# Graph attention on one core: two key blocks of scores in a row, then the sums of two blocks

## Chip, cores, metric

The kernel runs on one core of a Trainium2 chip. The metric is the device time of one execution in microseconds (us); lower is better. One core has TensorE (matrix products, into PSUM), VectorE, ScalarE, GpSimd (POOL in the profile) and the queues that issue DMAs, SyncE's (SP) among them.

## Reference

Four graph layers over 4096 nodes with 128 features, each followed by a residual and a layer norm. The change concerns the second layer, a masked attention with four heads of 32 features:

```
q, k, v = x @ Wq + bq, x @ Wk + bk, x @ Wv + bv      # (4096, 4 heads, 32)
attn  = q . k / sqrt(32)                             # per head, 4096 x 4096
e     = exp(attn) where adj != 0, else 0             # (softmax, its maximum taken off)
out   = (e @ v) / (row sum of e)
x_r   = x @ Ws + bs
beta  = sigmoid([out, x_r, out - x_r] @ Wb)
x     = layernorm(x + beta * x_r + (1 - beta) * out)
```

`adj` is a 4096 x 4096 matrix of zeros and ones in float32, symmetric, with about 1.6% ones. The other three layers use the same matrix in other ways and are not touched.

## The kernel before

`attention_unshifted` computes the second layer without taking the maximum off (a test on the sizes of q and k guards this). The queries are cut into 8 outer blocks of 512 (`NS`, index `I`), the keys into 32 blocks of 128 (`NT`, index `jb`). A list `seq` holds all 256 pairs (I, jb) in order.

For each pair there are two steps:

- `scores(I, jb)`: for two heads at a time, TensorE computes the transposed scores of 128 keys by 512 queries into a PSUM tile `ps` (pool `ps_s`, three buffers; a tile holds two heads; L1994). ScalarE takes the exp of the tile into the SBUF tile `e` (pool `ep`, three buffers; L2001). When all four heads are there, VectorE multiplies `e` with the mask, which it makes from a bfloat16 block `at` of the adjacency matrix (L2003).
- `sums(I, jb)`: TensorE multiplies the masked `e` with the values, which carry a column of ones for the row sums, and accumulates over the 32 key blocks in two PSUM tiles `pv` (pool `ps_v`; L2020). Two heads share a tile, one in its lower and one in its upper 64 partitions. A product of plain float32 appears in the profile as two instructions, so one key block has eight of them.

The order on every engine's queue is the order in which the program is written (`manual_schedule`); within it the framework picks the buffers and sets the waits. The main loop runs over n with `LEAD = 2`: it issues the scores of pair n + 2 and then the sums of pair n. TensorE's queue thus alternates: four score matmuls, eight sum matmuls. Other work is placed in the loop by hand:

- `load` (SyncE's queue, L1959) brings the mask block for four key blocks, one ahead, into one of two buffers.
- `row` (ScalarE's queue, L1970) loads half of an adjacency row block; `degree` (ScalarE, L1976) sums it, for the third layer; `look` (VectorE, L1985) tests some of these rows. They come at every fourth key block.
- `stack` (POOL's queue, L2181) brings keys and queries into the layout of the score matmuls. In the first outer block a one-element copy `pace` (POOL, L2127) on a masked `e` delays it.
- `ending(I)` finishes an outer block after its last sums. ScalarE copies the two `pv` tiles to SBUF (L2033); TensorE transposes them in two portions into tiles `pto` of the pool `ps_s` (L2043), one portion into each tile; VectorE divides (L2044 to L2050), forms the gate and the layer norm, with a few tiny functions on ScalarE. It is a generator: the loop takes one portion of it, `next(rest)`, after the sums of each following key block.

Of the kernel before, what the change touches and what calls it, by code (L numbers as in the profile page):

```python
# [1643 lines left out]
class Fast(Net):  # L1644
# [296 lines left out]
    def attention_unshifted(self, VA, KS, QS, at0, stack, R, wb):  # L1941

        nc, tc, N, NT, NS, D, X = self.nc, self.tc, self.N, self.NT, self.NS, self.D, self.X
        NH, C = 4, D // 4
        W = C + 1
        with ExitStack() as ctx:
            rot = ctx.enter_context(tc.tile_pool(name="rotf", bufs=1))
            natp = ctx.enter_context(tc.tile_pool(name="natf", bufs=2))
            atp = ctx.enter_context(tc.tile_pool(name="atf", bufs=1))
            ep = ctx.enter_context(tc.tile_pool(name="ef", bufs=3))  # L1950
            ps_s = ctx.enter_context(tc.tile_pool(name="ps_s", bufs=3, space=PSUM))
            ps_v = ctx.enter_context(tc.tile_pool(name="ps_v", bufs=1, space=PSUM))
            st = {("at", 0, 0): at0, "look": []}
# [3 lines left out]
            def load(I, J):  # L1957
                at = st["at", I, J] = ats[J % 2]
                nc.sync.dma_start(out=at, in_=self.block(I, J))  # L1959
# [3 lines left out]
            def row(n):  # L1963

                if n < len(halves):
                    i, k = halves[n]
                    h, c = N // 2, slice(k * N // 2, (k + 1) * N // 2)
                    st["row"] = n
                    st["nat"] = natp.tile([P, h], F32, tag="nat", name="nat")
                    nc.scalar.dma_start(out=st["nat"], in_=self.adj[i * P : (i + 1) * P, c])  # L1970

            def degree():
                n = st["row"]
                i, k = halves[n]
                nat = st["nat"]
                nc.scalar.activation(nat, nat, AF.Identity, accum_out=self.deg2[:, k, i : i + 1])  # L1976
                row(n + 1)
                if i % 4 > 1:
                    st["look"] = [nat[:, b * N // 4 : (b + 1) * N // 4] for b in range(2)]

            def look():

                if st["look"]:
                    a = st["look"].pop(0)
                    nc.vector.scalar_tensor_tensor(  # L1985
                        a, a, 0.0, a, op0=ALU.not_equal, op1=ALU.not_equal, accum_out=self.mark()
                    )

            def scores(I, jb):
                e = ep.tile([P, NH, S], F32, tag="e", name="e")  # L1990
                for h2 in range(0, NH, 2):
                    p = ps_s.tile([P, 2, S], F32, tag="s", name="ps")
                    for h in range(2):
                        nc.tensor.matmul(  # L1994
                            p[:, h, :],
                            lhsT=KS[:, h2 + h, jb * P : (jb + 1) * P],
                            rhs=QS[I % 2][:, h2 + h, :],
                            start=True,
                            stop=True,
                        )  # L2000
                    nc.scalar.activation(e[:, h2 : h2 + 2, :], p, AF.Exp)  # L2001
                at = st["at", I, jb // 4]
                nc.vector.scalar_tensor_tensor(  # L2003
                    e,
                    at[:, jb % 4, :].unsqueeze(1).to_broadcast([P, NH, S]),
                    0.0,
                    e,
                    op0=ALU.not_equal,
                    op1=ALU.mult,
                )  # L2010
                st["e", I, jb] = e

            def sums(I, jb):
                e = st.pop(("e", I, jb))
                if jb == 0:
                    st["po"] = [ps_v.tile([P, S], F32, tag=f"pv{a}", name=f"pv{a}") for a in range(2)]
                for h in range(NH):
                    g = 64 * (h % 2)
                    o = (jb * NH + h) * W
                    nc.tensor.matmul(  # L2020
                        st["po"][h // 2][g : g + 64, :],
                        lhsT=VA[:, o : o + 64],
                        rhs=e[:, h, :],
                        start=(jb == 0),
                        stop=(jb == NT - 1),
                        skip_group_check=True,
                    )
# [77 lines left out]
            seq = [(I, jb) for I in range(NS) for jb in range(NT)]  # L2105
            LEAD = 2
            rest = iter(())
            d = self.deg
            with tc.manual_schedule():
                load(0, 1)  # L2110
                row(0)
                for n in range(-LEAD, len(seq)):
                    if n + LEAD < len(seq):
                        I, jb = seq[n + LEAD]
                        if jb % 4 == 0:
                            m = n + LEAD + 4
                            if m < len(seq) and (m // 4) > 1:
                                load(m // NT, m % NT // 4)

                        if jb % 4 == 3 and (I or jb > 8) or I == NS - 1 and jb in (13, 17):  # L2120
                            look()
                            degree()
                        if I == 0 and jb % 4 == 0 and jb // 4 + 2 < NS:
                            c = jb // 4 + 2
                            if jb:

                                nc.gpsimd.tensor_copy(pace, st["e", I, jb - 1][0:1, 0, 0:1])  # L2127
                            stack(1, KS[:, :, c * S : (c + 1) * S], c)
                        if jb == 3 and 0 < I < NS - 1:
                            stack(0, QS[(I + 1) % 2], I + 1)  # L2130
                        scores(I, jb)
                        if n == -LEAD:
                            nc.scalar.preload_act_table_set("natural_log_exp_and_others")
                        if jb % 4 < 2:
                            look()
                    if n >= 0:
                        I, jb = seq[n]
                        sums(I, jb)
                        next(rest, None)
                        if jb == NT - 1:  # L2140
                            for _ in rest:
                                pass
                            rest = ending(I)
                            next(rest)
                for _ in range(2):
                    look()
                for _ in rest:
                    pass
# [430 lines left out]
```

## Time and profile before

| | |
|---|---|
| median of 3 runs | 2046.96 us (2040.15 to 2052.23) |
| profiled execution, its own time | 2050.21 us |
| its span in the trace | 2048.4 us |
| TensorE busy, of the span | 1900.9 us, 93% |
| VectorE busy | 1736.6 us, 85% |
| ScalarE busy | 1328.8 us, 65% |
| mean granted TensorE clock | 0.954 |

The stage of the change reaches from about 790 to 1590 us of the span. In the profile PE is TensorE's matmuls, PEld its weight loads, DVE is VectorE, ACT is ScalarE, SP is SyncE; a trailing q marks a queue's own instruction, such as the issue of a DMA. L1994 is line 1994 of the kernel. A group's row gives the tiles written and read, the shapes, the number of instructions, their busy time, the mean length of one, and how long the engine was idle just before them and on whose account. The ends of matmuls are modelled, so starts are the firmer numbers for TensorE.

### The profile page before, as it was taken

The numbers are of one execution on the slowest core, as the hardware profiler recorded it, in microseconds if no ns is written. First come the engines' busy times: TensorE is split into PE (matmuls) and PEld (weight loads), VectorE is DVE, ScalarE is ACT, GpSimd is POOL, SyncE is SP. The second block draws the span as 40 slices with busy tenths as digits, with TensorE's granted clock in tenths as the row PEclk, the third lists the DMA queues.
The fourth block names the chain that finished last, engine by engine and source line by source line (L and its number), as shares of the span: only waits on it lengthen the run. The fifth ranks groups of instructions, "written<-read, shape, count | busy, mean of one in ns | idle before, by whom it ended". The sixth has DMA issues, their size and how long they took to land.

```text
span 2048.4 us, 23818 instructions
## 1 busy us (share of the span) xinstructions
PE 1900.9 (93%) x8648; PEld 978.9 (48%) x8680; DVE 1736.6 (85%) x2685; ACT 1328.8 (65%) x1681; POOL 171.4 (8%) x269
## 2 busy tenths in 40 slices
PE   4789999999997788999999999999999799999997
PEld 4257766666666454333333333333333344444443
DVE  6579999998988946789999999999999777778986
ACT  5589999999997723777787777778787322210000
POOL 2211112111100221300000000000000000000000
PEclk8569999999999998999999999999999999999999
DMA  3488989899825977853535453545343799934441
GB/s 101 49 139 147 155 167 157 155 163 168 144 93 191 363 277 223 199 152 132 144 124 146 136 150 134 144 133 155 124 139 118 290 396 373 340 116 156 155 148 43
DMA packets 138064, 350.22 MB, mean 171 GB/s; under 512 B 13196, under 2 KB 56364, under 8 KB 125648
## 3 DMA queue, kind: packets, MB, share of 16 engines
q1 hardware_dynamic: 82944, 230.27, 32.3%
q0 software_dynamic: 45632, 50.69, 20.1%
q10 hardware_dynamic: 9360, 67.64, 9.9%
q8 instruction: 70, 1.15, 0.2%
q14 instruction: 58, 0.48, 0.1%
HBM read 371.54 MB, written 44.12 MB: 203 GB/s over the span
## 4 chain that ended last, share of the span: by engine, by line
PE 49%; DVE 24%; ACT 16%; DMA 6%; issue 4%; SPq 0%; POOL 0%; another core or an unknown queue 0%; ACTq 0%; DVEq 0%; POOLq 0%
PE pv L2020 11%; PE pa L1573 9%; DVE e L2003 9%; PE pa L2372 7%; PE ps L1994 6%; ACT e L2001 4%; PE pz L1775 3%; DMA up<-adjb 3%; DVE nat L1985 2%; ACT w L1792 2%; PE pi L1859 2%; PE pj L1874 2%; ACT s L1815 2%; ACT y L1811 2%; ACT y L1807 1%
## 5 line engine op out<-in xcount | busy, mean ns | idle before, releaser
L2003 DVE SCALAR_TENSOR_TENSOR e<-at,e 128x2048 f32<-128x2048 bf16 x256 | 582.6, 2286 | 77.3 <-ACT e L2001 76.7
L2001 ACT ACTIVATE e<-ps 128x1024 f32<-128x1024 f32 x512 | 492.9, 1024 | 150.6 <-PE ps L1994 121.6
L2020 PE MATMUL pv<-e,VA 128*64 128x512 f32 x2048 | 497.6, 607 | 6.7 <-DVE e L2003 5.7
L1994 PE MATMUL ps<-QS,KS 128*128 128x512 f32 x1024 | 314.8, 425 | 9.1 <-ACT e L2001 8.5
L1994 PEld LDWEIGHTS ps<-QS,KS 128*128 128x128 f32 x1024 | 170.9, 189 | 236.5 <-ACT e L2001 177.4
L2020 PEld LDWEIGHTS pv<-e,VA 128*64 128x64 f32 x2048 | 125.1, 136 | 250.2 <-issue 214.4
L1573 PE MATMUL pa<-w,Y 128*128 128x512 f32 x448 | 195.3, 594 | 0.0
L1775 PE MATMUL pz<-HT 128*128 128x512 f32 x288 | 171.8, 681 | 15.0 <-DVE w L1847 10.2
L1570 DVE SCALAR_TENSOR_TENSOR w<-rho,col,ring 128x512 f32<-128x512 f32 x224 | 162.7, 746 | 22.3 <-PE pa L1573 9.7
L2372 PE MATMUL pa<-ring,Y 128*128 128x512 bf16 x750 | 172.7, 384 | 8.7 <-ACT Y L2353 6.7
L1859 PE MATMUL pi<-HA,w 128*128 128x129 f32 x1152 | 156.6, 286 | 6.5 <-ACT s L1815 5.3
L1859 PEld LDWEIGHTS pi<-HA,w 128*128 128x128 f32 x1152 | 143.3, 199 | 18.2 <-issue 10.2
L1573 PEld LDWEIGHTS pa<-w,Y 128*128 128x128 f32 x448 | 83.8, 190 | 105.9 <-issue 80.3
L1976 ACT ACTIVATE nat<-nat 128x2048 f32<-128x2048 f32 x64 | 122.6, 1915 | 2.8 <-DMA nat<-in_adj_dram 2.8
L1874 PE MATMUL pj<-HA,w 128*128 128x129 f32 x896 | 120.7, 293 | 3.4 <-DVE X L1888 2.4
L2372 PEld LDWEIGHTS <-Y 128*128 128x128 bf16 x768 | 75.4, 99 | 100.9 <-ACT Y L2353 9.7
L1784 DVE TENSOR_SCALAR t<-pz 128x512 f32<-128x512 f32 x144 | 93.6, 682 | 30.2 <-PE pz L1778 30.2
L1874 PEld LDWEIGHTS pj<-HA,w 128*128 128x128 f32 x896 | 112.8, 205 | 11.2 <-issue 6.8
L1823 DVE SCALAR_TENSOR_TENSOR t<-t,s 128x2048 f32<-128x2048 f32 x36 | 82.3, 2286 | 13.4 <-ACT s L1815 13.4
L1792 ACT ACTIVATE w<-di,dr 128x512 f32<-128x512 f32 x144 | 90.6, 707 | 1.5 <-DMA di<-rows 1.5
L2336 DVE SCALAR_TENSOR_TENSOR nat<-nat 128x2048 f32<-128x2048 f32 x32 | 73.1, 2287 | 20.5 <-DMA nat<-in_adj_dram 20.5
L1847 DVE TENSOR_TENSOR w<-w,ptz 128x512 f32<-128x512 f32 x112 | 73.4, 681 | 18.7 <-PE ptz L1842 17.3
(410 smaller groups left out, 2343.1 us busy)
## 6 DMA issues: line engine op xcount, KB each, us to landing
nat<-in_adj_dram ACTq DMA_DIRECT2D x64, 1024.0 KB, 5.1
ring<-adjb SPq DMA_DIRECT2D x128, 512.0 KB, 4.7
ad<-in_adj_dram SPq DMA_DIRECT2D x36, 1024.0 KB, 9.4
adjb<-in_adj_dram POOLq DMA_DIRECT2D x64, 512.0 KB, 11.4
nat<-in_adj_dram SPq DMA_DIRECT2D x32, 1024.0 KB, 7.5
at<-adjb SPq DMA_DIRECT2D x63, 512.0 KB, 3.5
low<-adjb SPq DMA_DIRECT2D x36, 512.0 KB, 5.1
up<-adjb SPq DMA_DIRECT2D x28, 512.0 KB, 6.6
```

Source lines behind the costliest of these rows:

```text
L1570: nc.vector.scalar_tensor_tensor(w, rho[:, I * S : (I + 1) * S], col[:, 0, j : j + 1], at[:, jb, :], op0=ALU.max, op1=ALU.mult)
L1573: nc.tensor.matmul(pa, lhsT=F[:, j, :], rhs=w, start=False, stop=(j == NT - 1), skip_group_check=True)
L1775: nc.tensor.matmul(pz, lhsT=HT[:, j * P : (j + 1) * P], rhs=HT[:, I * S : (I + 1) * S], start=True, stop=False)
L1792: nc.scalar.activation(w[:, jb, :], st[p]["d"][k], AF.Sigmoid, bias=dr[:, 4 * J + jb : 4 * J + jb + 1])
L1859: nc.tensor.matmul(row[I, "po"][ib // 2][:, ib % 2, :], lhsT=st[p]["w0"][:, jb, ib * P : (ib + 1) * P], rhs=HA[:, 4 * J + jb, :], start=False,
L1874: nc.tensor.matmul(pj[:, a, :], lhsT=st[p]["w1"][:, ib, jb * P : (jb + 1) * P], rhs=HA[:, 4 * I + ib, :], start=(ib == 0), stop=(ib == 3),)
L1976: nc.scalar.activation(nat, nat, AF.Identity, accum_out=self.deg2[:, k, i : i + 1])
L1994: nc.tensor.matmul(p[:, h, :], lhsT=KS[:, h2 + h, jb * P : (jb + 1) * P], rhs=QS[I % 2][:, h2 + h, :], start=True, stop=True,)
L2001: nc.scalar.activation(e[:, h2 : h2 + 2, :], p, AF.Exp)
L2003: nc.vector.scalar_tensor_tensor(e, at[:, jb % 4, :].unsqueeze(1).to_broadcast([P, NH, S]), 0.0, e, op0=ALU.not_equal, op1=ALU.mult,)
L2020: nc.tensor.matmul(st["po"][h // 2][g : g + 64, :], lhsT=VA[:, o : o + 64], rhs=e[:, h, :], start=(jb == 0), stop=(jb == NT - 1), skip_gro ...
L2372: nc.tensor.matmul(st["pa"], lhsT=parts[k][:, j, :], rhs=at[:, jb, :], start=(I > 0 and j == k == 0), stop=(j == NT - 1 and k == 2), skip_ ...
```

## The change

The loop over n takes steps of two. One pass issues the scores of pairs n + 2 and n + 3, each with the loads, row sums and looks that stood ahead of and behind it, and then the sums of pairs n and n + 1. The pool of the masked exps gets a fourth buffer. `next(rest)` is still taken twice for two key blocks: once between the two score blocks (after that with even jb), and once after the two blocks of sums.

```
-            ep = ctx.enter_context(tc.tile_pool(name="ef", bufs=3))
+            ep = ctx.enter_context(tc.tile_pool(name="ef", bufs=4))
...
-                for n in range(-LEAD, len(seq)):
-                    if n + LEAD < len(seq):
-                        I, jb = seq[n + LEAD]
+                for n in range(-LEAD, len(seq), 2):
+                    for I, jb in seq[n + LEAD : n + LEAD + 2]:
                         if jb % 4 == 0:
-                            m = n + LEAD + 4
+                            m = I * NT + jb + 4
                             if m < len(seq) and (m // 4) > 1:
                                 load(m // NT, m % NT // 4)
...
                         scores(I, jb)
-                        if n == -LEAD:
+                        if I == jb == 0:
                             nc.scalar.preload_act_table_set("natural_log_exp_and_others")
                         if jb % 4 < 2:
                             look()
-                    if n >= 0:
-                        I, jb = seq[n]
+                        if n >= 0 and jb % 2 == 0:
+                            next(rest, None)
+                    if n < 0:
+                        continue
+                    for I, jb in seq[n : n + 2]:
                         sums(I, jb)
-                        next(rest, None)
-                        if jb == NT - 1:
-                            for _ in rest:
-                                pass
-                            rest = ending(I)
-                            next(rest)
+                    next(rest, None)
+                    if jb == NT - 1:
+                        for _ in rest:
+                            pass
+                        rest = ending(I)
+                        next(rest)
```

## Prediction

> **What bounds the kernel now.** The change lies in the second layer, so I first took the busy time by stretches to see which engine that stage runs on, then the costliest groups, then TensorE's timeline in a steady stretch. The table of stretches gives the stage as 790 to 1590 us of the span; one row stands for its middle (columns: stretch, length, then busy time and instructions by engine, TensorE's clock, DMA share, GB/s):
>
> ```profile
> core 0: us, PE busy (x) PEld busy (x) DVE busy (x) ACT busy (x) POOL busy (x), PEclk, DMA share, GB/s
> 1100.00:1200.00 100.00, 99.24 (x401) 38.19 (x400) 92.54 (x110) 79.23 (x91) 2.15 (x4) 1.00 0.46 138
> ```
>
> TensorE is never idle, at full clock; VectorE has 7% left, ScalarE 21%, the DMA engines half. But a busy TensorE need not be at its best pace. The groups (engine, operation, tiles, count, busy us, mean ns of one, idle before):
>
> ```profile
> L2003 DVE SCALAR_TENSOR_TENSOR e<-at,e 128x2048 f32<-128x2048 bf16 x256 | 582.6, 2286 | 77.3 <-ACT e L2001 76.7
> L2001 ACT ACTIVATE e<-ps 128x1024 f32<-128x1024 f32 x512 | 492.9, 1024 | 150.6 <-PE ps L1994 121.6
> L2020 PE MATMUL pv<-e,VA 128*64 128x512 f32 x2048 | 497.6, 607 | 6.7 <-DVE e L2003 5.7
> L1994 PE MATMUL ps<-QS,KS 128*128 128x512 f32 x1024 | 314.8, 425 | 9.1 <-ACT e L2001 8.5
> ```
>
> A key block is thus four score matmuls, two exps, one masking and eight sum matmuls. TensorE's timeline (start, length) shows the beat, and narrow windows of it the starts inside one beat:
>
> ```profile
> 1284.38 1.94 PE L2020 MATMUL pv<-e,VA 128*64 128x512 f32 x8
> 1286.25 1.20 PE L1994 MATMUL ps<-QS,KS 128*128 128x512 f32 x4
> 1287.38 1.94 PE L2020 MATMUL pv<-e,VA 128*64 128x512 f32 x8
> ...
> 1284.86 0.60 PE L2020 MATMUL pv<-e,VA 128*64 128x512 f32 x2
> 1285.72 0.60 PE L2020 MATMUL pv<-e,VA 128*64 128x512 f32 x2
> 1286.25 0.50 PE L1994 MATMUL ps<-QS,KS 128*128 128x512 f32 x1
> 1286.59 0.63 PE L1994 MATMUL ps<-QS,KS 128*128 128x512 f32 x2
> 1286.82 0.63 PE L1994 MATMUL ps<-QS,KS 128*128 128x512 f32 x2
> 1287.06 0.40 PE L1994 MATMUL ps<-QS,KS 128*128 128x512 f32 x1
> ```
>
> One block is 3.00 us, sums start to sums start. Within it a score follows a score after 0.235 us and a pair of sums a pair after 0.43. Around each turn it is slower: first to second score 0.34, last score to sums 0.32, first to second pair of sums 0.48, last pair to scores 0.53. Against the plain steps (0.235, 0.235, 0.43, 0.43) that is 0.105 + 0.085 + 0.05 + 0.10 = **0.34 us for each round of two turns**.
>
> An outer row block (32 key blocks) takes 98.35 us (sums at 1177.05 and 1275.40 us stand at the same place), so 2.35 over 32 x 3.00: 0.97 at jb 3 and 5, where the transposes of `ending` run, and the rest small stalls at jb 13, 21, 25 and 29, where VectorE or ScalarE is late (3.22, 3.28, 3.19 and 3.74 us for a block).
>
> **What the Trainium skill says.** TensorEngine Tiling (Array Packing), Key Properties: changing the tiling mode drains TensorE. Scores use 128 columns, sums 64, so each turn is such a change; the 0.34 us agrees with it. PSUM — Partial Sum Buffer, The four PSUM rules: one matmul output fills at most one of 8 banks. A score tile of 2 x 512 f32 is two banks; three of them and the two sums are all eight, so no fourth score buffer exists. ScalarE: Activation LUTs, What ACT_TABLE_LOAD costs: an ACTIVATE with immediates takes 186 + 0.833 N ns, and neighbours overlap by about 93. For N = 1024 that is 1039; the trace has 1024, and 0.92 from start to start.
>
> **The change part by part.** Time 0 is the first score matmul of a two-block group.
>
> *Turns.* 128 groups make 128 rounds of turns instead of 256: 0.34 us less per group. The trace has such a double run of sums at the stage's end:
>
> ```profile
> 1583.16 3.65 PE L2020 MATMUL pv<-e,VA 128*64 128x512 f32 x16
> ```
>
> 3.65 - 1.94 = 1.71 for the second block, four plain steps. Without a wait, eight scores start at 0, 0.34, then every 0.235, the seventh at 1.515 and the eighth at 1.75, sums at 2.07, and first sums to next scores are 1.87 + 1.71 = 3.58. A group would be 5.65 us against 6.00.
>
> *The new wait.* A group fills four score tiles, and there are three. The seventh matmul (fourth tile) needs the exp of the group's own first tile. That exp starts when the second score ends: 0.77 us after the first one in the steady beat (ScalarE's timeline has one at 1287.02, for scores at 1286.25). It takes 1.02. From an exp's end to the matmul is 0.05: at the stage's start six scores ran in a row and the seventh waited:
>
> ```profile
> 793.32 1.94 ACT L2001 ACTIVATE e<-ps 128x1024 f32<-128x1024 f32 x2
> ...
> 794.39 0.72 PE L1994 MATMUL ps<-QS,KS 128*128 128x512 f32 x2 [2.84 <-ACT e L2001]
> ```
>
> 793.32 + 1.02 = 794.34, matmul at 794.39. So the seventh goes at 0.77 + 1.02 + 0.05 = 1.84, not 1.515. After such a wait the next score comes 0.34 later, not 0.235; a score block at 1200.28 that waited for an exp is longer by 0.2 for this:
>
> ```profile
> 1200.28 1.40 PE L1994 MATMUL ps<-QS,KS 128*128 128x512 f32 x4
> ```
>
> Eighth at 2.18, sums at 2.50, group 2.50 + 3.58 = **6.08 us against 6.00**. All eight sum matmuls of each block queue behind this wait. The turns saved (0.34) and the wait (0.325 + 0.105 = 0.43) cancel: 128 x 0.08 = **+10 us**.
>
> *Fourth exp buffer and longer lead.* Exps of blocks n+2 and n+3 take the buffers whose sums ended the group before. Masking the second block starts at 2.75 + 2.28 = 5.03 or later (a look, 1.15, or a step of `ending`, some 0.4, may come between); its sums start at 6.08 + 2.50 + 1.87 = 10.45. Even with two looks (5.03 + 1.15 + 0.4 + 2.28 = 8.9) there is 1.5 us in hand. I let half of the small stalls go: 1.4 us per row block at most, so -0.7 in six of them; in the first, ScalarE's waits for a buffer at jb 7 to 13 (four blocks of 3.72) go in part, -2; in the last, with two more degree rows, -1. In all **-7 us**. The trace doesn't show how waits fall in the new order: from -16 (all gone) to +8, since ScalarE's queue waits for a row's DMA issue until VectorE has looked (0.47 lost after the row at 1198.50), and now an exp that comes later stops scores at once.
>
> *Transposes of `ending`.* They move from behind the sums to between the two score blocks. Their tile takes the third score buffer. So the fifth score matmul waits for exp one (1.84), the seventh for exp two (0.92 later, 2.76), sums at 3.42: +0.92 over a plain group, transposes included. In the next group the second transposes want a buffer at about 1.1; the earliest free is that of exp one at 1.84; then score five at some 2.4, seven at 3.0, sums at 3.6: +1.1. Together 2.0 us a row block against 0.97 before, so +1.05, seven times: **+7 us**. Below: +0. Above: if the next group had to take the very buffer of the transposes, which VectorE frees only after masking block jb 3: the masking before it ends near 5.7, the small steps at 6.0, the row sum on ScalarE holds the exps until 6.4, masking 6.5 to 8.8, products 9.4. The groups would be 9.4 and 8.2 instead of 6.08, 5.5 us a row block. Against it: at 1200.28 scores started while the first transposes' tile was still to be read (products 1203.15 to 1203.81), so the order of buffers isn't a fixed round.
>
> *Orders that stay.* Exps, row sums, copies of the sums and row DMAs keep their order on ScalarE, maskings, looks and `ending`'s steps on VectorE; SP's block loads and POOL's stacking DMAs stand at the same score blocks, and each block's transfer (3.5 us) has four blocks' time as before: nothing. A group with a row sum: exps 0.77 to 2.7, row sum to 4.5, exps to 6.4, before the next first exp at 6.85: nothing. At the stage's end the last sums hang on the last masking; counted from the scores of block 30 they start at 8.8 us, both before (1587.84 - 1579.04) and by the steps above: nothing. The table load moves nowhere.
>
> Sum: +10 - 7 + 7 = +10, and +2 for the row DMAs that I think likely: **+12 us** on the profiled execution's 2050.2 us (span 2048.4). The median of the runs, 2047.0, is 3.3 lower, so I say **2059 us**.
>
> **Rivals.**
> - *Plain cancellation* (chance 0.25): all small stalls vanish, -16, against +10 and +5: -1, some 2046. For it: 1.5 us in hand at every masking. Against: VectorE at 92.5% and ScalarE's row DMAs.
> - *Transposes hold the scores up* (0.17): 5.5 - 0.97 = 4.5 us, seven times, +32, with +10: 2047 + 42 = 2089. For it: only three score buffers. Against: the start at 1200.28.
> - *Faster: the wait does not bind* (0.10). Its place is the seventh score matmul; it decides if the first exp is through by 1.515, that is in 0.70 us where the row says 1.02, or if the tiles' waits fall elsewhere. Then 0.35 x 128 = -45, of which VectorE (91 of 98.35 us busy a row block) leaves about -35: 2012. The measured exp speaks against it.
> - That the groups aren't formed as written I don't expect: TensorE's queue follows the written order throughout.
>
> **How the numbers follow.** The forecast gets 0.48. About 0.5% (10 us) is what a measurement of this kernel can tell from no change. Faster: 0.10 and the tail of the cancellation, 0.11. Same: most of the cancellation and a fifth of the forecast, 0.28. Slower: the rest, 0.61. The range reaches from the forecast's low end, 2059 - 12 - 10 = 2037, which takes in the cancellation, to the transposes' rival at 2090; the faster case is left out.
>
> **What would show it.** Right: TensorE alternates eight scores and sixteen sums; the seventh score starts 1.8 us after the first, released by ScalarE's exp; groups take 6.1 us; TensorE's busy share in the stage falls by some 3%. Transposes: groups at jb 2 and 4 near 7 us, not 9. Wrong: groups of 5.7 us (no wait), or plain groups over 6.3 (ScalarE late), or masking as the releaser of most sums.

## The result and the profile after

The changed kernel takes 2064.4 us (median of 6 runs, 2060.8 to 2068.1) against 2047.6 before; the ratio is 1.0082 (95% interval 1.0063 to 1.0101). That is 17 us more, where the prediction had 12, from 2047.0 to 2059, within its range. The interval leaves 1 out: the kernel is slower, by less than 1%.

The profiled execution has a span of 2059.0 us, only 10.6 more. The stage itself tells more: from the first score matmul to the end of the last sums it grew from 799.9 us (789.9 to 1589.8) to 817.5 (783.6 to 1601.1), by 17.6. What stands ahead of it, with the same code, happened to be 6.3 us shorter in this execution. So below I compare the stage, and in it one row block (32 key blocks), measured from the first transposes of one `ending` to those of the next: 98.37 us before, 101.27 after. A group means the work of one pass of the new loop, eight score and sixteen sum matmuls; a plain group is one without transposes and without a stall of its own.

The busy time of a middle stretch (columns as before the change):

```profile
1100.00:1200.00 100.00, 94.76 (x390) 38.77 (x388) 90.49 (x105) 76.45 (x86) 2.15 (x4) 1.00 0.43 133
```

TensorE, which stood still for under 1% of this stretch (99.24 of 100 us busy), now does so for 5%, at full clock still. The costliest groups on the page of the changed kernel:

```profile
L2003 DVE SCALAR_TENSOR_TENSOR e<-at,e 128x2048 f32<-128x2048 bf16 x256 | 583.2, 2287 | 93.3 <-ACT e L2001 92.4
L2001 ACT ACTIVATE e<-ps 128x1024 f32<-128x1024 f32 x512 | 488.5, 1029 | 158.2 <-PE ps L1994 145.8
L2020 PE MATMUL pv<-e,VA 128*64 128x512 f32 x2048 | 468.7, 599 | 0.9 <-DVE e L2003 0.9
L1994 PE MATMUL ps<-QS,KS 128*128 128x512 f32 x1024 | 312.5, 425 | 40.9 <-ACT e L2001 39.8
```

Two readings: the sums' busy time fell by 29 us (fewer turns, since busy time covers the slow starts), and the idle time ahead of the scores rose from 9.1 to 40.9 us, nearly all ended by an exp (L2001). Work and number of instructions are the same. A plain group on TensorE's timeline:

```profile
1236.50 3.65 PE L2020 MATMUL pv<-e,VA 128*64 128x512 f32 x16
1240.09 1.66 PE L1994 MATMUL ps<-QS,KS 128*128 128x512 f32 x6
1241.93 0.73 PE L1994 MATMUL ps<-QS,KS 128*128 128x512 f32 x2 [0.18 <-ACT e L2001]
1242.59 0.65 PE L2020 MATMUL pv<-e,VA 128*64 128x512 f32 x2
```

Six scores run, then the seventh waits for an exp: it starts 1.84 us after the first, the sums 2.50 after it, and the group takes 6.09 us. The 0.18 us in brackets is only the idle part of the 0.43 us lost; the rest hides in the modelled length of the sixth matmul and in the slow start after the wait. TensorE's waits over 900 to 1500 us, after:

```profile
PE ps L1994 <- ACT e L2001: 25.9, 94, 1.2
PE pto L2043 <- ACT e L2001: 4.2, 6, 0.7
```

Before, this view has one line, sums behind the masking (3.7 us in 13 waits). The two groups after a row block's end:

```profile
1194.67 1.19 PE L1994 MATMUL ps<-QS,KS 128*128 128x512 f32 x4
1195.69 0.60 PE L2043 MATMUL pto<-ident,ev 128*128 128x128 f32 x4
1196.50 0.73 PE L1994 MATMUL ps<-QS,KS 128*128 128x512 f32 x2 [0.21 <-ACT e L2001]
1197.42 0.73 PE L1994 MATMUL ps<-QS,KS 128*128 128x512 f32 x2 [0.18 <-ACT e L2001]
1198.08 3.65 PE L2020 MATMUL pv<-e,VA 128*64 128x512 f32 x16
1201.67 1.20 PE L1994 MATMUL ps<-QS,KS 128*128 128x512 f32 x4
1203.57 0.66 PE L2043 MATMUL pto<-ident,ev 128*128 128x128 f32 x4 [0.70 <-ACT e L2001]
1204.48 1.20 PE L1994 MATMUL ps<-QS,KS 128*128 128x512 f32 x4 [0.26 <-ACT e L2001]
1205.62 3.65 PE L2020 MATMUL pv<-e,VA 128*64 128x512 f32 x16
1209.20 2.57 PE L1994 MATMUL ps<-QS,KS 128*128 128x512 f32 x8
```

They take 7.00 and 7.53 us, from first score to first score: the transposes' tile holds one of three score buffers, so in the first group the fifth and the seventh score wait, and in the second the transposes and the fifth score.

### The profile page after: what moved, and what is told of

The parts are those of the page before. It is cut to its first block, busy times and chain, and to the rows that moved or that the text cites. A ratio compares the mean times of both kernels' runs of the same rounds, so it can differ in the third digit from the quotient of the medians.

```text
span 2059.0 us, 23824 instructions
## 1 busy us (share of the span) xinstructions
PE 1886.0 (92%) x8680; PEld 986.3 (48%) x8680; DVE 1738.8 (84%) x2685; ACT 1324.4 (64%) x1681; POOL 170.2 (8%) x269
## 4 chain that ended last, share of the span: by engine, by line
PE 50%; DVE 20%; ACT 18%; DMA 7%; issue 4%; SPq 0%; ACTq 0%; POOL 0%; DVEq 0%; POOLq 0%
PE pv L2020 12%; PE pa L1573 9%; ACT e L2001 7%; DVE e L2003 7%; PE pa L2374 7%; PE ps L1994 5%; PE pz L1775 3%; DMA up<-adjb 3%; ACT w L1792 3%; PE pi L1859 2%; PE pj L1874 2%; DVE nat L1985 2%; ACT s L1815 1%; PE pz L1778 1%; DVE t L1823 1%
## 5 line engine op out<-in xcount | busy, mean ns | idle before, releaser
L2001 ACT ACTIVATE e<-ps 128x1024 f32<-128x1024 f32 x512 | 488.5, 1029 | 158.2 <-PE ps L1994 145.8
L2020 PE MATMUL pv<-e,VA 128*64 128x512 f32 x2048 | 468.7, 599 | 0.9 <-DVE e L2003 0.9
L1994 PE MATMUL ps<-QS,KS 128*128 128x512 f32 x1024 | 312.5, 425 | 40.9 <-ACT e L2001 39.8
L2020 PEld LDWEIGHTS pv<-e,VA 128*64 128x64 f32 x2048 | 136.1, 137 | 268.2 <-issue 260.3
L1874 PE MATMUL pj<-HA,w 128*128 128x129 f32 x896 | 116.1, 285 | 0.6 <-DVE w L1847 0.6
L1874 PEld LDWEIGHTS pj<-HA,w 128*128 128x128 f32 x896 | 108.5, 198 | 8.2 <-issue 7.0
```

The source lines that it names most:

```text
L1874: nc.tensor.matmul(pj[:, a, :], lhsT=st[p]["w1"][:, ib, jb * P : (jb + 1) * P], rhs=HA[:, 4 * I + ib, :], start=(ib == 0), stop=(ib == 3),)
L1994: nc.tensor.matmul(p[:, h, :], lhsT=KS[:, h2 + h, jb * P : (jb + 1) * P], rhs=QS[I % 2][:, h2 + h, :], start=True, stop=True,)
L2020: nc.tensor.matmul(st["po"][h // 2][g : g + 64, :], lhsT=VA[:, o : o + 64], rhs=e[:, h, :], start=(jb == 0), stop=(jb == NT - 1), skip_gro ...
```

## The experiments

The question was where the saved turns went. Theory: to a wait for a score buffer. Rivals: VectorE, busy 91 of 98 us in a row block, lets nothing more through; or the fourth exp buffer decides. All row blocks below are from the traces.

| kernel | median us | ratio to before | row block us |
|---|---|---|---|
| before | 2047 to 2050 | 1 | 98.37 |
| the change | 2064.4 | 1.0082 [1.0063, 1.0101] | 101.27 |
| one-bank tiles, groups of two | 2037.8 | 0.9943 [0.9928, 0.9959] | 98.15 |
| one-bank tiles, order of before | 2045.3 | 0.9990 [0.9976, 1.0004] | 98.44 |
| four exp buffers, order of before | 2045.0 | 0.9983 [0.9973, 0.9993] | 98.38 |
| change, ending's portions behind the sums | 2118.7 | 1.0335 [1.0302, 1.0368] | 110 to 111 |
| change, two score buffers | 2217.7 | 1.0824 [1.0791, 1.0856] | 118 to 122 |
| change, three exp buffers | 2076.6 | 1.0140 [1.0111, 1.0170] | 102.7 |
| change, small functions later | 2058.7 | 1.0042 [1.0030, 1.0054] | 100.05 |
| change, short looks | 2055.6 | 1.0032 [1.0019, 1.0046] | 100.07 |
| three tiles in a row | 2079.6 | 1.0140 [1.0119, 1.0162] | 101 to 106 |
| one-bank, later functions | 2028.6 | 0.9907 [0.9882, 0.9932] | 96.43 |
| the same, short looks | 2013.1 | 0.9836 [0.9800, 0.9873] | 94.33 |
| one-bank, later functions, three row buffers | 2021.1 | 0.9850 [0.9826, 0.9873] | 95.39 |

**The wait taken away: one-bank score tiles.**

```
-            ps_s = ... tc.tile_pool(name="ps_s", bufs=3, space=PSUM)
+            ps_s = ... tc.tile_pool(name="ps_s", bufs=6, space=PSUM)
...
+                for h in range(NH):
+                    p = ps_s.tile([P, S], F32, tag="s", name="ps")
+                    nc.tensor.matmul(p, lhsT=KS[:, h, ...], rhs=QS[I % 2][:, h, :], ...)
+                    nc.scalar.activation(e[:, h, :], p, AF.Exp)
```

> The changed kernel, its score buffers cut in half: six tiles of one head (one bank) in place of three of two heads, and one exp of 512 for each. The seventh score of a group then needs the exp of the first head alone, which should end near 0.5 + 0.05 + 0.61 = 1.2 us, before the 1.5 at which the matmul is due. Theory (the wait for a score buffer took the gain): no wait, groups of about 5.65 us instead of 6.09, a row block of about 95 us instead of 101.3, so some 45 us below the changed kernel and 30 below the kernel before, near 2018 us. Rival (VectorE, busy 91 of 98 us a row block, lets nothing more through): sums then wait for the masking, groups stay near 6 us, and the time stays over 2045 us.

The transposes' tiles shrink to one bank as well. 2037.8 us, 27 below the change and 10 below the kernel before. (The 0.61 us for an exp of 512 columns comes from the prediction's formula; the median in this trace is 0.62.) TensorE's timeline of it:

```profile
1205.24 3.65 PE L2015 MATMUL pv<-e,VA 128*64 128x512 f32 x16
1208.82 2.17 PE L1993 MATMUL ps<-QS,KS 128*128 128x512 f32 x8
1210.93 0.65 PE L2015 MATMUL pv<-e,VA 128*64 128x512 f32 x2
```

Eight scores now run without a break, and a plain group takes 5.69 us (1205.24 to 1210.93), as worked out for a group without a wait. The groups with transposes fall as well, to 6.25 and 6.67. But the gain on the kernel before is a third of what I expected: a row block takes 98.15 us where sixteen plain groups would be 91, since seven groups are longer by 0.5 to 1.7. In the trace the whole gain lies in the first row block, which is 8.6 us shorter than before up to its first transposes (103.3 against 111.9); in each of the next six this order gains only 0.2 us. TensorE hardly idles any more ahead of plain groups; what is left are few and long waits (same view, same stretch):

```profile
PE ps L1993 <- ACT e L1996: 11.5, 12, 1.3
```

**Its control: the same tiles in the old order.** The edit is the one above, on the kernel before.

> The kernel before, with the same six one-bank score tiles and an exp for each head, its order of TensorE's work unchanged. It says what the smaller exps do by themselves. Theory: nothing waits for a score buffer in the old order, so within 5 us of the kernel before (2047), blocks of 3.00 us. Rival (smaller tiles are what pays): as far below the kernel before as the two-block kernel with one-bank tiles.

2045.3 us; the interval holds 1. Smaller tiles pay nothing by themselves; they pay only where the order needs a fourth tile. With the run above this shows the wait for a score buffer as what took the saved turns in the plain groups (6.09 to 5.69 us). It is not all that holds the row block: of the 6.4 us that sixteen such groups make, 3.1 came.

**The wait doubled: two score buffers.**

```
-            ps_s = ... tc.tile_pool(name="ps_s", bufs=3, space=PSUM)
+            ps_s = ... tc.tile_pool(name="ps_s", bufs=2, space=PSUM)
```

> The changed kernel with two score buffers in place of three: the suspected wait doubled. Theory: the fifth score matmul waits for the first exp (1.84 us) and the seventh for the second (2.76), so sums start at 3.42 instead of 2.50: plain groups of 7.0 us, 0.92 more in each of some 112 groups, and about 1 us more in each of 14 groups with transposes: near 2180 us. Rival (the score buffers don't set the pace): well under 50 us more.

2217.7 us, more than expected. Plain groups do what was worked out:

```profile
1245.56 1.20 PE L1994 MATMUL ps<-QS,KS 128*128 128x512 f32 x4
1247.41 0.72 PE L1994 MATMUL ps<-QS,KS 128*128 128x512 f32 x2 [0.65 <-ACT e L2001]
1248.33 0.74 PE L1994 MATMUL ps<-QS,KS 128*128 128x512 f32 x2 [0.19 <-ACT e L2001]
```

Fifth score at 1.85, seventh at 2.77, groups of 7.00 us. The surplus lies in the groups with transposes, which take 9.0 to 12.8 us: waits of 2 us there are followed by a halved TensorE clock (last section).

**The fourth exp buffer alone.**

```
-            ep = ctx.enter_context(tc.tile_pool(name="ef", bufs=3))
+            ep = ctx.enter_context(tc.tile_pool(name="ef", bufs=4))
```

> The kernel before with four buffers for the masked exps and nothing else of the change. Theory: only the four long blocks of the first row block (3.72 us), where ScalarE waited for a buffer, come down to 3.00: 3 us less, 2044; the small stalls at jb 13 to 29 stay, since they come from VectorE and ScalarE being late. Rival (the fourth buffer is what frees the small stalls): 1.4 us in each of seven row blocks as well, some 13 us less, 2034.

2045.0 us, 3.6 less. In the trace the first row block is 2.6 us shorter (111.9 to 109.3 us up to the first transposes), and the next six don't change. The small stalls of the old order do not come from the exp buffers.

**The change without it: three exp buffers** (the last edit, turned round, on the changed kernel).

> The changed order with three buffers for the masked exps, as before the change. The exps of a group's second block must then wait for the sums of the group's first. Theory: plain groups stay near 6.1 us, since these exps (4.4 to 6.3 us after the group's start) still end before the next group needs their score buffers; in the eight groups of a row block with a row sum on ScalarE they end near 8.2, and the next group loses about 1.3 us: some 70 us more, 2135. Rival (the fourth buffer is of no use to the new order): 2064.

2076.6 us, 12 more than the change and not 70. ScalarE's timeline shows why:

```profile
1240.08 1.94 ACT L2001 ACTIVATE e<-ps 128x1024 f32<-128x1024 f32 x2 [1.77 <-PE pv L2020]
...
1244.27 1.91 ACT L1976 ACTIVATE nat<-nat 128x2048 f32<-128x2048 f32 x1
1246.07 0.20 ACT L1976 ACTIVATION_READ_ACCUMULATOR nat<-nat 128x1 f32 x1
1246.16 1.94 ACT L2001 ACTIVATE e<-ps 128x1024 f32<-128x1024 f32 x2
```

The second block's exps do wait for the first block's sums. But the row sum stands ahead of them in the queue and runs inside that wait, where I had added it behind. The fourth buffer is worth 12 us to the new order, in the trace all of it in the groups with transposes and the one behind them (7.44, 7.60 and 7.00 us instead of 7.00, 7.53 and 6.09); it isn't what decides.

**VectorE relieved.** Most of the test of the adjacency rows is left out.

```
-  st["look"] = [nat[:, b * N // 4 : (b + 1) * N // 4] for b in range(2)]
+  st["look"] = [nat[:, b * N // 4 : b * N // 4 + 64] for b in range(2)]
```

> The changed kernel with VectorE relieved: each look tests 64 columns in place of 1024, so most of the test of the adjacency rows is left out. That takes about 8 us of VectorE's 91 in a row block. Theory (the wait for a score buffer sets the groups): plain groups stay at 6.09 us, only small stalls behind VectorE go; some 5 to 10 us less than the changed kernel, 2056. Rival (VectorE sets the groups): 8 us in each of eight row blocks, near 2000.

2055.6 us, 9 less than the change. Plain groups stay at 6.09 us although VectorE is at 84% (502 of 600 us). So in the change VectorE does not set the plain groups. What is won lies in two long groups, of 6.52 and 7.05 us, which fall to 6.16 and 6.09; they come up again below.

**The place of `ending`'s portions.**

```
-                        if n >= 0 and jb % 2 == 0:
-                            next(rest, None)
...
-                    next(rest, None)
+                    for _ in range(2):
+                        next(rest, None)
```

> The changed kernel with both portions of the outer block's ending taken after the two blocks of sums, none between the score blocks. Theory: the transposes no longer take a score buffer in the middle of a group; the two groups after a row block's end fall from 7.00 and 7.53 us to about 6.5 and 6.1, so 1.9 us in each of seven, some 13 us less than the changed kernel, near 2051. Rival (the place of the portions is without effect, the extra time of these groups is the transposes' own work): within 4 us of the changed kernel, 2064.

Both expectations fell: 2118.7 us. The transposes still take a score buffer ahead of the next scores (groups of 7.46 and 6.99), so nothing is won there. The loss is elsewhere: VectorE's step and ScalarE's small function of it now follow each other with no scores between them, and ScalarE, whose queue runs in order, stands at the function. ScalarE's and then TensorE's timeline:

```profile
1265.31 0.20 ACT L2069 ACTIVATE be<-be 128x4 f32<-128x4 f32 x1 [2.43 <-DVE be L2067]
1265.42 3.75 ACT L2001 ACTIVATE e<-ps 128x1024 f32<-128x1024 f32 x4
...
1266.47 0.73 PE L1994 MATMUL ps<-QS,KS 128*128 128x512 f32 x2 [2.83 <-ACT e L2001]
1267.14 5.35 PE L2020 MATMUL pv<-e,VA 128*64 128x512 f32 x16
```

Four exps queue behind a function of 0.2 us, the seventh score waits 2.83 us for the first of them, and the sums after it take 5.35 us instead of 3.65.

**The same cause in the change.** This pointed back at the long groups of 7.05 and 6.53 us in the changed kernel. ScalarE and TensorE at one of them:

```profile
1259.44 0.20 ACT L2087 ACTIVATE rs<-rs 128x4 f32<-128x4 f32 x1 [2.61 <-DVE rs L2083]
...
1261.18 0.73 PE L1994 MATMUL ps<-QS,KS 128*128 128x512 f32 x2 [1.14 <-ACT e L2001]
```

The edit, also ahead of the gate's exp:

```
                 yield
+                yield
                 nc.scalar.activation(rs, rs, AF.Ln)
```

> The changed kernel with one portion more between VectorE's step and ScalarE's small functions of it, at both places in the ending (exp of the gate, logarithm of the variance), so that ScalarE's queue no longer stands at them with exps of scores behind. Theory: the long groups of 7.05 and 6.53 us in every row block fall to about 6.2; 1.2 us in seven row blocks, some 8 us less than the changed kernel, near 2056 us. Rival (these groups are long because VectorE is late with its masking): unchanged within 4 us, 2064.

2058.7 us, 6 less. From sums to sums the two groups take 6.13 and 6.09, the one that now holds the logarithm 6.20 instead of 6.09, and ScalarE's waits for `rs` and `be` are gone from its list. A row block is 1.2 us shorter, as expected; the median shows 6 of the expected 8 us.

**Three tiles in a row.** `scores` and `sums` are split in half blocks of two heads, issued three at a time, scores four half blocks ahead.

```
+                for n in range(0, len(units), 3):
+                    for _ in range(3):
+                        one_score()
+                    for I, jb, half in units[n : n + 3]:
+                        sums(I, jb, half)
...
```

> Groups of three score tiles (a block and a half, six score matmuls) and then the sums of three half blocks, with the three two-bank buffers and the four exp buffers of the changed kernel. No score then needs a buffer of its own group. Theory: no wait, and 0.34 us of turns for a block and a half: six scores and twelve sums take 4.33 us, 2.89 a block against 3.00 before and 3.04 in the changed kernel; a row block of about 96 us with the stalls that VectorE makes, some 15 us below the kernel before, 2033. Rival (longer runs don't pay in themselves, whatever the buffers): at or above the kernel before, 2047 or more.

```profile
1230.54 1.66 PE L1996 MATMUL ps<-QS,KS 128*128 128x512 f32 x6
1232.13 2.80 PE L2023 MATMUL pv<-e,VA 128*64 128x512 f32 x12
1234.86 1.67 PE L1996 MATMUL ps<-QS,KS 128*128 128x512 f32 x6
...
1291.05 1.08 PE L2023 MATMUL pv<-e,VA 128*64 128x512 f32 x4 [1.39 <-DVE e L2007]
```

Plain groups are 4.32 us for a block and a half, as worked out, with no wait for a buffer; yet 2079.6 us in all. Sums wait for the masking, and scores for exps that came late. The lead in half blocks leaves masking less time than the order of before; that this is the cause is argued, not shown. It is not the whole: here too ScalarE stands at the small functions, 4.40 us for `rs` at 1067.62, and behind that wait TensorE runs at half clock:

```profile
1067.62 0.20 ACT L2090 ACTIVATE rs<-rs 128x4 f32<-128x4 f32 x1 [4.40 <-DVE rs L2086]
...
1074.50:1078.00 3.50, 3.50 (x10) 0.98 (x10) 3.50 (x2) 1.26 (x2) 0.00 (x0) 0.50 0.14 26
```

**Wait and small functions both removed.** One-bank tiles and the extra portions:

> The changed kernel with six one-bank score tiles and the same extra portions ahead of ScalarE's small functions. With one-bank tiles alone, plain groups take 5.69 us but a row block still 98.15, since five groups in it are longer by 0.7 to 1.7. Theory: two of these (7.1 and 7.4 us) come from ScalarE standing at a small function that VectorE has not fed; they fall by some 2 us together, a row block to 96, the time to some 2023 us. Rival (VectorE, now the fullest engine with 91 us in a row block, is what holds the long groups): the stall only moves to the sums behind their masking, within 5 us of one-bank tiles alone, 2038.

2028.6 us, 9 below one-bank tiles alone (expected 15). Then the same with short looks, most of the test of the rows left out:

> The changed kernel with one-bank score tiles, the later small functions and the same short looks (most of the test of the rows left out). Theory: once the wait for a buffer is gone, VectorE is the next bound; relieved of 8 us a row block, it lets the groups run at 5.7 us: a row block of 93 to 94 us instead of 96.4, some 22 us less, near 2006. Rival (the rest of the long groups has another cause, such as the transposes or ScalarE's work): within 5 us of the same kernel with full looks, 2029.

2013.1 us: 15 less (expected 22), where the change as it stands gave 9 for the same relief. VectorE's masking in these two, 900 to 1400 us, without and with short looks:

```profile
L1998 DVE SCALAR_TENSOR_TENSOR e<-at,e 128x2048 f32<-128x2048 bf16 x166 | 377.0, 2284 | 27.4 <-ACT e L1996 26.5
```

```profile
L1998 DVE SCALAR_TENSOR_TENSOR e<-at,e 128x2048 f32<-128x2048 bf16 x170 | 386.7, 2285 | 57.1 <-ACT e L1996 57.1
```

With full looks the masking waits for an exp in only 27 of 500 us, so VectorE has little left once the buffer is there. But a look also holds up the issue of a row's DMA on ScalarE's queue, and with it the exps behind (three waits of 0.5 us in each row block, which are gone with short looks); short looks take away both, so this run alone can't tell which of them gave the 15 us.

**A third buffer for the adjacency rows**, on top of one-bank tiles and later functions:

```
-            natp = ctx.enter_context(tc.tile_pool(name="natf", bufs=2))
+            natp = ctx.enter_context(tc.tile_pool(name="natf", bufs=3))
```

> One-bank score tiles and later small functions, and three buffers for the adjacency rows in place of two, so that the issue of a row's DMA on ScalarE's queue no longer waits for VectorE's look at an earlier row. Theory: the exps that stood behind this wait come 0.5 to 1 us earlier in four groups of a row block, which shortens groups of 6.37 us by about 0.4: 1.2 us in each row block, some 10 us less than with two buffers, 2019. Rival (VectorE is full there, so the exps' earlier start only lengthens their masking's queue): within 4 us, 2028.

2021.1 us, ratio 0.985: with the whole computation, 43 us below the change and some 29 below the kernel before. The row block of 95.39 us is 1.04 shorter, near the 1.2 expected, though in two groups and not in four (6.37 to 5.92 and to 5.79): the DMA issue that waited on ScalarE's queue for a look had held exps back. VectorE's work is the same here, so half of the 2.1 us that short looks won in a row block was this wait and not a full VectorE; for the other half VectorE's load remains the likely cause, not shown apart from its order.

## Why the prediction was right, and where it was off

- *Turns and the new wait.* Right to a hundredth: 0.34 us saved per group, seventh score at 1.84, sums at 2.50, group 6.09 (predicted 6.08). Removing the wait gave groups of 5.69 (5.65).
- *VectorE as cover.* Right that it had time in hand in plain groups: sums hardly wait for masking after the change (0.9 us in all). The 1.5 us itself was not measured.
- *Transposes.* Predicted 7.0 and 7.2 us for the two groups, measured 7.00 and 7.53. The fifth score of the second group came at 2.81 us and not 2.4: it took the buffer of the second exp, not an earlier one. Against before that is 2.35 - 0.97 = 1.38 us a row block instead of 1.05. The order of buffers isn't a fixed round, as argued, so the 9 us groups of the rival did not come.
- *The small stalls* were the mis-sized term. I let half of them go (-0.7 us a row block). They stayed in size (1.38 us before, some 1.5 after) but changed their cause: ScalarE's small functions of VectorE's results now stop the exp that the seventh score needs. Before, ScalarE stood 1.48 us at `rs` as well, and no block in the 8 us behind it was longer than 3.00 us by more than 0.2. I had counted a row's DMA issue as such a wait, not these functions. The first row block gained 3.6 us; at 0.09 us a group its plain groups alone would have cost it some 1.4, so its stalls fell by some 5 and not by the 2 assumed. The fourth exp buffer alone gives 2.6 of it; the rest stays open.
- *The sum.* Six row blocks at +2.90 (16 x 0.09 + 1.38 + 0.1) give 17.4, the first piece up to the first transposes -3.6, the last row block +3.8: 17.6 against 12 predicted. That it came so near is in part luck: the row blocks lost more than forecast, and the first piece, which gained more, hid some of it. The 2 us added for the row DMAs are shown by no run of the changed kernel.
- *The rivals.* Plain cancellation fell because the small stalls did not vanish; the faster case fell with the wait.

## What to carry to other kernels

A longer run of one kind of matmul needs as many result buffers as the run fills, less what the reader frees while it lasts; work out the start of the first matmul that needs a buffer of its own run, and compare the wait with the turns that it saves. If no memory is left for a further buffer, smaller tiles may free the first one in time. Then look down every in-order queue that now feeds this wait: a tiny instruction that waits for a late engine holds up all that stands behind it.

## What was not expected of the hardware

TensorE's clock halves after waits that look short. In the kernel with `ending`'s portions behind the sums, the seventh score waited 2.83 us and started at 1266.47. The busy time of the 3.4 us ahead of the fall and of the 3.4 us behind it:

```profile
1264.07:1267.48 3.41, 1.00 (x4) 0.50 (x6) 1.31 (x3) 2.17 (x4) 0.00 (x0) 1.00 0.49 193
1267.48:1270.90 3.42, 3.42 (x10) 0.97 (x8) 3.42 (x2) 1.68 (x2) 0.00 (x0) 0.50 0.09 37
```

TensorE was busy for 1.00 us of the first stretch, and the granted clock of the second is 0.50; the sums in it take 5.35 us instead of 3.65. With two score buffers a wait of 2.06 us, after shorter ones, had the same 5.35 us behind it. The Trainium skill (TensorE: Matmul & The Clock Gate, What's actually happening) puts the fall to half clock after an idle window of about 3.4 us; here the single waits were shorter than that, so a window that is partly idle can be enough. How large the idle part must be was not measured. The plain groups of the change, with 0.18 us idle in 6.09, never lost the clock.
